# Decoder layer: both rotation products of the paired queries on GpSimd, in pieces of 512 columns, and one of the seven products a place further ahead

## The chip, the core and the metric

The kernel runs on one core of a Trainium2 chip. The metric is the device time of one execution in microseconds (us), the median of several runs. The core's engines work side by side, each through its own queue of instructions in order: TensorE (PE) multiplies matrices, VectorE (DVE), ScalarE (ACT) and GpSimd (POOL) work on elements, and SyncE (SP) mainly starts DMA transfers.

## The reference

One pre-norm decoder layer in fp32 for four sequences of 512 tokens with 512 features. Cut to what matters here:

```python
def rope(v):                       # per head of 64 features
    return v * cos + rotate_half(v) * sin    # rotate_half: (-upper half, lower half)

h  = layernorm(x)
xq = rope((h @ wq).reshape(B, T, 32, 64))    # 32 query heads
xk = rope((h @ wk).reshape(B, T, 8, 64))     # 8 key heads, each for 4 query heads
xv = (h @ wv).reshape(B, T, 8, 64)
p  = softmax(causal(xq @ xk.T / 8))
x  = x + (p @ xv).reshape(B, T, 2048) @ wo

x  = x + quant_dequant(layernorm(x)) @ quant_dequant(ctx_2048).T   # fp8 blocks, per sequence
x  = x + moe(layernorm(x))         # 8 experts of 704, 256 rows each, and a shared expert
```

The quantization takes a scale for each row and block of 128 features, rounds to fp8 and multiplies back.

## The kernel before

**Stages.** The layer norms of the first sequence and the weights come first. Then the attention runs as one loop over 80 rounds, each with two score steps, 160 in all (n = 0 to 159), about 40 for each of the four sequences (b = 0 to 3). The projections, output projections, cross product with the context, and the second and third layer norms of one sequence are pushed in between the score steps of this and the following sequences. The shared expert and the eight experts follow behind the attention, from about 1040 us on in the profile.

**Who decides the order.** The instruction stream is written by Python code that keeps a time model of its own (`Clock`, line 29) and plans against it. A piece of work that may be pushed in is a generator, a job (`add`, line 1239), with the score step from which it may be done, the step by which it must be done and a wish (`want`) that sorts the jobs. What a job yields is its own estimate of the PE time issued, or a condition: `"at"` means not before a planned time, `"done"` not before its own last instruction is planned to have ended, and `"dve", time, cost` that the next instruction is a DVE one of that cost, issued only where the planned DVE queue has room for it. `Fill` (line 1346) picks among the jobs: `upto` fills the gap between two groups of PE work, `need` finishes a job at once where a score step needs its result (line 1498 for the queries). Since everything is planned against the model, a change in one job reorders what is issued behind it.

**The loop.** In each round of the main loop (lines 1750 to 1762), `scores(n + 1)` issues the score products (tile `sc`) one step ahead into four PSUM banks, DVE masks them and takes the maximum (`pm`, `mn`), ACT takes the exponential. `weighted` multiplies finished, transposed probabilities by the values (`av`). `work.upto` fills in jobs. `turned` transposes the probabilities on PE (`pt`) through the same four banks, and DVE or ACT copies them out (`pT`). So `pt` waits until DVE has read the scores out of the bank, and the next `sc` until the copies `pT` are out.

**Other jobs that the text names.** `psk`, `psv`: projections of keys and values. `aT`: the attention's output, scaled by POOL with the reciprocal sums (`rrb`), of which `rr` and `prr` are steps. `py`: products of the output projection (`wo` by `aT`), summed by DVE into `y` and `acc`, and later the product with the context. `qm_x`, `qv_x`, `qq_x`: DVE's steps of the quantization of a row block, which PE then transposes (`ptr_h`) into `h2T`; `qq_c` and `ptr_c` are the same for the context. `T`: differences and sums of the normed rows, which the seven products need.

**Paired queries.** For sequences 1 to 3, `job_q(b, m)` (line 741) computes the queries of four heads at once, m = 0 to 7, 24 such pairs in all. A pair is one tile `t1q` of 128 x 2 x 512: two planes (i = 0, 1), each holding two heads of 64 rows over 512 tokens, of which the score steps read one plane at a time (`qTs[b, 2 * m + i]`). The 2 x 2 block product is done by seven products of 128x256 instead of eight, over prepared sums of weights (`wq`) and rows (`T`), in four PSUM tiles `psq_b_m_0` to `_3`. They lie in the three banks of the kind "mm", which the other projections use too; the first tile is kept open (`kept_open`) until its second half is written. ACT copies the first product into the pair's tile and DVE adds the others to it.

Then comes the rotation. With X the pair, `rt[:, 0]` the cosines and `rt[:, 1]` the signed sines (each 128 x 512, the same for both planes), the kernel forms R2 = X * rt1 (tile `t2q`) and X * rt0 (in place, in `t1q`). `swap` (line 677) exchanges the half-heads of R2 by four DMAs on SP's queue into tile `tsq`, and POOL adds `tsq` to `t1q`, one plane at a time, which makes the plane ready for the scores. There is one tile `t2q` and one `tsq`, so one pair turns at a time; the set `turning` holds it, and `need` finishes a pair that stands in the way first. Queries of sequence 0 (`job_q1`) and the keys (`job_k`) go through `rotated` (line 682), which works on single 128x512 tiles and is the same in both kernels.

All instructions are recorded at the helper's line, L284, so the profile is read by tiles.

Of the kernel before, what the change touches and what calls it, by code (L numbers as in the profile page):

```python
# [11 lines left out]
ALU = mybir.AluOpType  # L12
# [296 lines left out]
def decoder_layer(  # L309
# [18 lines left out]
    clock = Clock()  # L328
    nc = Engines(clock, tc.nc)
# [56 lines left out]
    def places(kind):  # L386

        shut = [
            (place_free(kind, i), clock.used[held[kind, i]][1] if (kind, i) in held else 0, i)
            for i in range(PLACES[kind])  # L390
            if not clock.used.get(held.get((kind, i)), ((kind, i) in held,))[0]
            and (kind, i) not in kept_open
        ]
        return [i for *_, i in sorted(shut)]

    def bank(kind, name, dt=F32, i=None):
        if i is None:
            i = places(kind)[0]
        t = psum.tile([P, 512], dt, tag=f"{kind}{i}", name=name)
        held[kind, i] = t.tensor.name  # L400
        return t
# [218 lines left out]
    gpsimd = nc.gpsimd.tensor_tensor  # L620
# [56 lines left out]
    def swap(ts, t2):  # L677
        for i in range(4):
            o = i ^ 1
            nc.sync.dma_start(out=ts[i * HH : (i + 1) * HH], in_=t2[o * HH : (o + 1) * HH])  # L680
# [39 lines left out]
    turning = set()  # L720

    def pair_tile(b, m):
        return am1.tile([P, 2, T], F32, tag="qT", bufs=4, name=f"t1q_{b}_{m}")

    def turn_tiles(b, m):
        t2 = pj.tile([P, 2, T], F32, tag="t2", name=f"t2q_{b}_{m}")
        ts = pj.tile([P, 2, T], F32, tag="ts", name=f"tsq_{b}_{m}")
        return t2, ts
# [12 lines left out]
    def job_q(b, m):  # L741

        w = wts["q", m]
        a11, a12, s3, a22, s1, s2, s4 = (w[:, i] for i in range(7))
        t1, t2, t3, t4, b11, b21, b22 = Ts[b]

        def product(ps, i, w, x):
            for k in range(2):
                nc.tensor.matmul(
                    ps[:, i * WB : (i + 1) * WB], w[:, k, :], x[:, k, :], start=k == 0, stop=k == 1  # L750
                )

        name = f"q_{b}_{m}"
        add2 = nc.vector.tensor_tensor
        p0 = bank("mm", f"ps{name}_0")
        mine = next(x for x in held if held[x] == p0.tensor.name)
        kept_open.add(mine)
        product(p0, 0, a11, b11)
        Xp = pair_tile(b, m)
        X = Xp.rearrange("p i (h t) -> p (i h) t", h=2)  # L760
        nc.scalar.copy(X[:, 3, :], p0[:, 0:WB])
        yield 860
        p1 = bank("mm", f"ps{name}_1")
        product(p1, 0, a12, b21)
        yield 860
        product(p1, 1, s2, t2)
        halves = lambda ps: ps.rearrange("p (h t) -> p h t", h=2)
        twice = lambda x: x.unsqueeze(1).to_broadcast([P, 2, WB])
        add2(X[:, 0:2, :], halves(p1), twice(X[:, 3, :]), ALU.add)
        yield 860  # L770
        product(p0, 1, s3, t3)
        kept_open.discard(mine)
        add2(X[:, 2, :], p0[:, WB:T], X[:, 1, :], ALU.add)
        yield 860
        p2 = bank("mm", f"ps{name}_2")
        product(p2, 0, s1, t1)
        add2(X[:, 1:4:2, :], twice(p2[:, 0:WB]), X[:, 1:3, :], ALU.add)
        yield 860
        p3 = bank("mm", f"ps{name}_3")
        product(p3, 0, s4, b22)  # L780
        yield 860
        product(p3, 1, a22, t4)
        over["ps" + name] = clock.at
        add2(X[:, 1:3, :], halves(p3), X[:, 1:3, :], ALU.add)
        rot = lambda i: rt[:, i, :].unsqueeze(1).to_broadcast([P, 2, T])
        yield 860
        while turning:
            yield -0.05
        turning.add(m)
        R2, ts = turn_tiles(b, m)  # L790
        yield "dve", clock.begun(R2.tensor.name), 1.2
        nc.vector.tensor_tensor(R2, Xp, rot(1), ALU.mult)
        yield "dve", 0, 1.2
        nc.vector.tensor_tensor(Xp, Xp, rot(0), ALU.mult)
        yield "at", clock.wrote(R2)
        swap(ts, R2)
        yield "done"
        for i in range(2):
            gpsimd(Xp[:, i, :], Xp[:, i, :], ts[:, i, :], ALU.add)
            qTs[b, 2 * m + i] = Xp[:, i, :]  # L800
        turning.discard(m)

    def job_v(b, c, j):
        if not j:
            vs[b, c] = am1.tile([P, TB, HV], F32, tag="v", bufs=3, name=f"v_{b}_{c}")
        ps = bank("mm", f"psv_{b}_{c}_{j}")
        for i in range(2):
            t0 = (2 * j + i) * P
            for k in range(KC):
                nc.tensor.matmul(  # L810
                    ps[:, i * HV : (i + 1) * HV],
                    hTs[b][:, k, t0 : t0 + P],
                    wts["v", c][:, k, :],
                    start=(k == 0),
                    stop=(k == KC - 1),
                )
                if k % 2 and (i, k) != (1, KC - 1):
                    yield 860
        nc.scalar.copy(
            vs[b, c][:, 2 * j : 2 * j + 2, :],  # L820
            ps.rearrange("p (i n) -> p i n", i=2),
        )
        yield 860
# [413 lines left out]
    jobs = []  # L1237

    def add(due, cost, key, gen, *after, want=None):

        jobs.append(Job(due, cost, key, gen, after, want))

    MM4, MM7 = 4 * 860, 7 * 860
    for b in range(B):
        z = b * SPB
# [18 lines left out]
        for c in range(2):  # L1264
            for j in range(2):
                if b or c or j:
                    add(
                        z - 16, MM4, ("v", b, c, j), job_v(b, c, j), ("h", b), ("wv", b, c),
                        want=z - 4 + 0.8 * (2 * c + j),
                    )  # L1270
        if not b:
            for m in range(2 * NG):
# [2 lines left out]
        for a in range(NG):  # L1275
            za = z + 10 * a
            if za:
# [8 lines left out]
                    want=za - 4.5 - 2 * early,  # L1286
                )
            for r, due in enumerate((-17, -12)):
                m = 2 * a + r
                want = 4 * r - 3.2 if a < NG - 1 or b == B - 1 else 1.6 * r - 3.5  # L1290
# [28 lines left out]
            if not n:  # L1319
# [8 lines left out]
                want=za + ((21, 21, 17, 16.5) if b < B - 1 else (22, 19.5, 18, 16.5))[a],  # L1328
# [17 lines left out]
    class Fill:  # L1346
# [91 lines left out]
        def need(self, n, key):  # L1438

            while self.now is not None and key not in over:  # L1440
                self.now = self.step(self.now, n)
            if key in over:
                return
            if isinstance(key, str):
                key = (key[2], *map(int, key.split("_")[1:]))
            job = next(job for job in jobs if job.key == key)
            for k in job.after:
                self.need(n, k)
            jobs.remove(job)
            self.urgent = True  # L1450
            while job:
                for other in [x for x in jobs if turning and x.key[0] == "q" and x.key[2] in turning]:
                    jobs.remove(other)
                    while other:
                        other = self.step(other, n) or (jobs.remove(other) or other if other in jobs else None)
                job = self.step(job, n) or (jobs.remove(job) or job if job in jobs else None)
            self.urgent = False
# [191 lines left out]
    rt = pj.tile([P, 2, T], F32, name="rt")  # L1649
# [521 lines left out]
    _, b, j = units[-1]  # L2171
    for k, lo, hi, py in down_last(gTs[b], se["w"][1], j, f"ys_{b}_{j}"):
        i = b * TB + j + k
# [63 lines left out]
```

## Time and profile before

| | |
|---|---|
| median of 3 runs | 1524.3 us (1522.41 to 1524.41) |
| the profiled execution's own time | 1527.95 us |
| its span in the trace | 1526.2 us |
| its mean granted TensorE clock | 0.995 |
| PE busy | 1500.5 us (98%) |
| DVE, ACT, POOL busy | 928.6, 611.8, 598.8 us |
| PE's share of the chain that ended last | 91% |
| DVE's products `t2q<-t1q,rt`, 128x1024, 24 times | 32.6 us |
| DVE's products `t1q<-t1q,rt`, 128x1024, 24 times | 33.9 us |
| POOL's sums `t1q<-t1q,tsq`, 128x512, 64 times | 84.2 us |

How to read it: the profile is of one execution on the chip. Busy times are sums over an engine's instructions; the span runs from the first to the last recorded instruction, and the profiled execution's own time is a little longer than it. "A <- B" for a wait means that engine A stood idle until B released it; the releaser is inferred and is the last of several. The granted clock is the share of full speed at which TensorE was allowed to run. The 64 sums on POOL are 48 of the paired queries and 16 of sequence 0.

### The profile page before, as it was taken

The numbers are of one execution on the slowest core, as the hardware profiler recorded it, in microseconds if no ns is written. First come the engines' busy times: TensorE is split into PE (matmuls) and PEld (weight loads), VectorE is DVE, ScalarE is ACT, GpSimd is POOL, SyncE is SP. The second block draws the span as 40 slices with busy tenths as digits, with TensorE's granted clock in tenths as the row PEclk, the third lists the DMA queues.
The fourth block names the chain that finished last, engine by engine and source line by source line (L and its number), as shares of the span: only waits on it lengthen the run. The fifth ranks groups of instructions, "written<-read, shape, count | busy, mean of one in ns | idle before, by whom it ended". The sixth has DMA issues, their size and how long they took to land.

```text
span 1526.2 us, 23127 instructions
## 1 busy us (share of the span) xinstructions
PE 1500.5 (98%) x7742; PEld 961.8 (63%) x7745; DVE 928.6 (61%) x2666; ACT 611.8 (40%) x1756; POOL 598.8 (39%) x617
## 2 busy tenths in 40 slices
PE   8999999999999999999999999999999999999999
PEld 5655465756556675655657565655456788868864
DVE  4365635558777666978657687765855554434434
ACT  3554544545455544545455455455111322111100
POOL 2342431103253231334323224423644267776723
PEclk9999999999999999999999999999999999999999
DMA  5575552435352553534334353454051353466526
GB/s 138 161 232 179 172 157 70 139 108 137 88 142 56 156 175 99 146 94 135 111 108 155 112 146 87 131 167 154 27 184 46 108 187 134 160 218 214 201 70 220
DMA packets 120872, 210.73 MB, mean 138 GB/s; under 512 B 16689, under 2 KB 48689, under 8 KB 120241
## 3 DMA queue, kind: packets, MB, share of 16 engines
q1 hardware_dynamic: 116256, 199.03, 43.2%
q0 software_dynamic: 2560, 8.39, 1.6%
q10 hardware_dynamic: 1936, 1.84, 0.4%
q8 instruction: 61, 1.00, 0.3%
q14 instruction: 59, 0.48, 0.1%
HBM read 144.98 MB, written 34.87 MB: 118 GB/s over the span
## 4 chain that ended last, share of the span: by engine, by line
PE 91%; DVE 6%; ACT 1%; issue 1%; DMA 1%; POOL 0%; SPq 0%; DVEq 0%; ACTq 0%; POOLq 0%
PE py L284 14%; PE psq L284 12%; PE p_s L284 9%; PE p_e L284 9%; PE sc L284 9%; PE av L284 9%; PE pt L284 8%; PE ys L284 5%; PE epy L284 5%; PE psv L284 4%; PE psk L284 3%; PE ptr_h L284 1%; ACT pm L284 1%; DVE pm L284 1%; DMA wq<-wsum 1%
## 5 line engine op out<-in xcount | busy, mean ns | idle before, releaser
L284 ACT ACTIVATE pm<-pm,mn 128x256 f32<-128x256 f32 (+3 forms) x512 | 280.8, 549 | 248.7 <-DVE mn L284 248.7
L284 DVE CUSTOM_DVE_ANT_0 pm<-sc,mask 128x256 f32<-128x256 f32 (+3 forms) x512 | 216.7, 486 | 53.4 <-PE sc L284 53.0
L284 PE MATMUL py<-wo,aT 128*128 128x512 f32 x512 | 242.3, 605 | 0.8 <-DVE acc L284 0.8
L284 ACT COPY pT<-pt 128x512 f32<-128x512 f32 (+3 forms) x325 | 130.7, 450 | 136.2 <-PE pt L284 122.5
L284 POOL TENSOR_TENSOR aT<-aT,rrb 128x512 f32<-128x512 f32 x64 | 86.5, 1366 | 245.2 <-DMA rrb<-rrd 208.6
L284 PE MATMUL sc<-kT,t1q 64*128 64x128 f32 (+3 forms) x1024 | 165.1, 451 | 4.8 <-DVE mn L284 2.8
L284 PEld LDWEIGHTS pt<-ident,pm 128*128 128x128 f32 x1280 | 144.4, 141 | 32.1 <-issue 21.1
L284 POOL TENSOR_TENSOR t1q<-t1q,tsq 128x512 f32<-128x512 f32 x64 | 84.2, 1332 | 198.7 <-DMA tsq<-t2q 139.2
L284 PE MATMUL pt<-ident,pm 128*128 128x128 f32 x1280 | 155.3, 274 | 3.7 <-DVE mn L284 3.5
L284 PE MATMUL av<-pT,v 128*64 128x512 f32 (+3 forms) x1024 | 152.4, 439 | 0.2 <-ACT pT L284 0.2
L284 PEld LDWEIGHTS py<-wo,aT 128*128 128x128 f32 x512 | 92.5, 192 | 94.8 <-issue 87.2
L284 DVE COPY pT<-pt 128x256 f32<-128x256 f32 (+3 forms) x187 | 78.6, 444 | 102.4 <-PE pt L284 64.9
L284 PEld LDWEIGHTS av<-pT,v 128*64 128x64 f32 x1024 | 68.4, 136 | 106.8 <-issue 95.2
L284 PE MATMUL psq<-hT,wq 128*128 128x256 f32 (+1 forms) x416 | 132.1, 450 | 0.4 <-ACT h2T L284 0.2
L284 POOL TENSOR_TENSOR acc<-acc,y 128x512 f32<-128x512 f32 x64 | 83.1, 1302 | 124.6 <-DVE y L284 122.7
L284 PEld LDWEIGHTS sc<-kT,t1q 64*128 64x128 f32 x1024 | 85.9, 188 | 70.9 <-issue 44.8
L284 PEld LDWEIGHTS psq<-hT,wq 128*128 128x128 f32 x416 | 76.0, 190 | 36.0 <-issue 27.3
L284 ACT ACTIVATION_READ_ACCUMULATOR pm<-pm,mn 128x1 f32 x512 | 95.5, 187 | 0.0
L284 PE MATMUL psq<-T,wq 128*128 128x256 f32 x384 | 94.7, 383 | 0.8 <-ACT t1q L284 0.8
L284 DVE TENSOR_TENSOR t1q<-psq,t1q 128x512 f32<-128x512 f32 x96 | 59.8, 623 | 49.9 <-PE psq L284 44.0
L284 DVE TENSOR_TENSOR acc<-py,acc 128x512 f32<-128x512 f32 x64 | 43.9, 687 | 68.2 <-PE py L284 67.7
L284 PE MATMUL ys<-slot_s,gT 128*128 128x512 f32 (+3 forms) x204 | 83.0, 588 | 1.7 <-DVE gT L284 1.7
(239 smaller groups left out, 2304.7 us busy)
## 6 DMA issues: line engine op xcount, KB each, us to landing
wq<-wsum SPq DMA_DIRECT2D x24, 896.0 KB, 4.9
slot_e<-in_L_ffn_W_dram SPq DMA_DIRECT2D x16, 1280.0 KB, 8.6
rrb<-rrd SPq DMA_DIRECT2D x64, 256.0 KB, 4.2
wo<-in_L_attn_wo_dram SPq DMA_DIRECT2D x15, 1024.0 KB, 5.4
tsq<-t2q SPq DMA_DIRECT2D x96, 128.0 KB, 2.8
slot_e<-in_L_ffn_W_dram SPq DMA_DIRECT2D x8, 1408.0 KB, 6.2
kT<-t1k SPq DMA_DIRECT2D x60, 128.0 KB, 2.4
wsum<-wq SPq DMA_DIRECT2D x8, 896.0 KB, 4.2
```

Source lines behind the costliest of these rows:

```text
L284: got = call(*args, **kw)
```

## The change

The two rotation products of `job_q` go from DVE, one 128x1024 instruction each, to POOL, two 128x512 instructions each. The two for R2 are issued ahead of the swap, the two in place behind its DMAs. The conditions on room in DVE's queue fall away; the first product instead waits until the tile of R2 is planned to be free. Among the seven products the one of the first sums (s1 by t1, into `psq_2`) is issued one place further ahead, before the second product of the first tile (s3 by t3), so that the two sums which read them come together. The set `turning` names a pair by sequence and number in place of the number alone. The `want` of the value projections is written in another form with the same value.

```diff
         yield 860
+        p2 = bank("mm", f"ps{name}_2")
+        product(p2, 0, s1, t1)
+        yield 860
         product(p0, 1, s3, t3)
         kept_open.discard(mine)
         add2(X[:, 2, :], p0[:, WB:T], X[:, 1, :], ALU.add)
-        yield 860
-        p2 = bank("mm", f"ps{name}_2")
-        product(p2, 0, s1, t1)
         add2(X[:, 1:4:2, :], twice(p2[:, 0:WB]), X[:, 1:3, :], ALU.add)
...
         while turning:
             yield -0.05
-        turning.add(m)
+        turning.add((b, m))
         R2, ts = turn_tiles(b, m)
-        yield "dve", clock.begun(R2.tensor.name), 1.2
-        nc.vector.tensor_tensor(R2, Xp, rot(1), ALU.mult)
-        yield "dve", 0, 1.2
-        nc.vector.tensor_tensor(Xp, Xp, rot(0), ALU.mult)
+        yield "at", clock.begun(R2.tensor.name)
+        for i in range(2):
+            gpsimd(R2[:, i, :], Xp[:, i, :], rt[:, 1, :], ALU.mult)
         yield "at", clock.wrote(R2)
         swap(ts, R2)
+        for i in range(2):
+            gpsimd(Xp[:, i, :], Xp[:, i, :], rt[:, 0, :], ALU.mult)
         yield "done"
         for i in range(2):
             gpsimd(Xp[:, i, :], Xp[:, i, :], ts[:, i, :], ALU.add)
             qTs[b, 2 * m + i] = Xp[:, i, :]
-        turning.discard(m)
+        turning.discard((b, m))
...
-                        want=z - 4 + 0.8 * (2 * c + j),
+                        want=z - 4 + 0.8 * j + 1.6 * c,
...
-                for other in [x for x in jobs if turning and x.key[0] == "q" and x.key[2] in turning]:
+                for other in [x for x in jobs if turning and x.key[0] == "q" and x.key[1:] in turning]:
```

The changed program issues the same number of PE instructions as before. On DVE there are 48 products fewer and nine copies `pT` more, on ACT those nine copies fewer, on POOL 96 products more; SP issues as many DMAs. From the first paired query on (about 230 us) the order of the other work shifts with it.

## The prediction

> **What bounds the kernel now.** I read the busy shares first, then the chain that ended last, then what TensorE (PE) waits for, and only then the rows of the instructions that change.
>
> ```profile
> PE 1500.5 (98%) x7742; PEld 961.8 (63%) x7745; DVE 928.6 (61%) x2666; ACT 611.8 (40%) x1756; POOL 598.8 (39%) x617
> ...
> PE 91%; DVE 6%; ACT 1%; issue 1%; DMA 1%; POOL 0%; SPq 0%; DVEq 0%; ACTq 0%; POOLq 0%
> ```
>
> PE is busy for 1500.5 of 1526.2 us, so all its idle time is 25.7 us. VectorE (DVE) and GpSimd (POOL) have room on average, 61% and 39%. Taking 66 us from DVE therefore gives nothing by itself: only PE's waits can be won or lost. Most of those in the attention part end on DVE (columns: waiting engine and tile, releaser, total us, times, longest):
>
> ```profile
> PE pt L284 <- DVE mn L284: 3.5, 2, 2.2
> PE ptr_h L284 <- DVE qq_x L284: 3.1, 2, 2.0
> ...
> PE sc L284 <- DVE pT L284: 1.8, 1, 1.8
> ...
> ```
>
> The timeline at the longest of them shows whether the changed products stand in DVE's queue ahead of what PE waits for (start, duration, instruction, in brackets the idle time before it).
>
> ```profile
> 433.64 2.17 DVE L284 TENSOR_TENSOR t1q<-t1q,rt 128x1024 f32<-128x1024 f32 x1
> 438.67 3.10 PE L284 MATMUL pt<-ident,pm 128*128 128x128 f32 x16 [2.19 <-DVE mn L284]
> 703.27 1.21 DVE L284 TENSOR_TENSOR t2q<-t1q,rt 128x1024 f32<-128x1024 f32 x1
> 705.29 1.09 PE L284 MATMUL sc<-kT,t1q 64*128 64x512 f32 x3 [1.83 <-DVE pT L284]
> 734.82 0.40 PE L284 MATMUL ptr_h<-ident_b,qq_x 128*128 128x128 bf16 x4 [2.03 <-DVE qq_x L284]
> ```
>
> At 438 and 705 they do. A wait costs more than itself when the clock drops behind it. The table of windows shows one such drop (columns: window, length, then busy time of PE, weight load, DVE, ACT and POOL, granted clock, DMA share, GB/s):
>
> ```profile
> 440.00:444.00 4.00, 3.97 (x11) 2.31 (x12) 3.93 (x14) 3.39 (x12) 1.88 (x2) 0.57 0.48 162
> ```
>
> PE is busy for 3.97 of 4 us there, at a granted clock of 0.57: a loss of 1.7 us (0.43 x 4). The waits at 34, 438.67, 705.29 and 1108.58 have such a drop behind them, those at 106.60, 646.27 and 734.82 don't. The Trainium skill ("TensorE: Matmul & The Clock Gate", "What's actually happening") has the clock fall after an idle window of about 3.4 us; the trace shows it after 2.19 us, so here the measurement decides.
>
> **The change part by part.** The prices come from these rows (lines by form: busy us, mean ns, then idle time before; tile rows: min/median/max ns, first and last start).
>
> ```profile
> L284 DVE TENSOR_TENSOR t1q<-t1q,rt 128x1024 f32<-128x1024 f32 x24 | 33.9, 1413 | 0.4
> L284 POOL TENSOR_TENSOR t1q<-t1q,tsq 128x512 f32<-128x512 f32 x64 | 84.2, 1332 | 198.7 <-DMA tsq<-t2q 139.2 <-DVE t1q L284 26.0 <-DVE mn L284 20.7
> ...
> L284 DVE TENSOR_TENSOR t2q<-t1q,rt x24: 1159/1223/2309, 239.2 to 978.2; 128x1024 f32<-128x1024 f32 x24
> L284 POOL TENSOR_TENSOR t1q<-t1q,tsq x64: 1262/1276/2258, 27.2 to 985.8; 128x512 f32<-128x512 f32 x64
> ```
>
> *Moved work.* DVE loses 24 x 1.36 (the t2q products by form, 32.6 us busy) + 24 x 1.41 = 66.5 us. POOL gains 24 x 4 = 96 products of 128x512. No row shows a POOL multiplication of this shape; the nearest is its addition of the same shape and sources, 1.27, so 96 x 1.27 = 122 us. POOL is busy for 251 of the 810 us from 230 to 1040 where these pairs are rotated, so it has room. The second products (61 us) follow the issue of the swap; POOL stood idle for 139.2 us behind exactly that swap (tsq<-t2q), which hides them. The first products lie on the pair's path: 2 x 1.27 in place of 1.22, so 1.3 us later per pair.
>
> *DVE's waits.* In the program's order of the changed kernel the transposes of step 62 still follow the scores of step 63 with nothing between, but the 2.17 us product is no longer in DVE's queue ahead of them: -0.9 of the wait (2.19 less the 1.30 that the same bare order costs at 106.60), -1.7 of clock, and +1.0 because the scores of step 65, which had 5.5 us of output projection (py) before them, now follow bare: -1.6. At step 103 likewise: -1.2 (the product's 1.21), -1.7, +1.3 for a new bare place: -1.6.
>
> *The quantize waits.* Here the nearest rows speak against the change, since they show what POOL's work does to DVE's:
>
> ```profile
> 382.97 0.43 DVE L284 TENSOR_SCALAR qm_x<-qm_x 128x512 f32<-128x512 f32 x1
> 383.43 0.69 DVE L284 TENSOR_TENSOR qv_x<-qv_x,qm_x 128x512 f32<-128x512 f32 x1
> ...
> 730.04 1.38 DVE L284 TENSOR_SCALAR qm_x<-qm_x 128x512 f32<-128x512 f32 x1
> 731.45 1.63 DVE L284 TENSOR_TENSOR qv_x<-qv_x,qm_x 128x512 f32<-128x512 f32 x1
> ```
>
> The first pair ran alone, the second beside POOL: 0.95 us more each. By the order, though, the PE work between a quantized row and its transposes grows for most of them (12.3 to 19.9 us and 10.2 to 20.5 us for two of batch 3; 10.0 unchanged for the first of batch 0), so the waits 2.0 + 0.7 (at 734.82) + 0.7 + 0.3 + 0.7 = 4.4 us should go: -4.4. For one or two quantize instructions slowed where the distance did not grow I add +1.0 (bounds 0 and 4, four such instructions). The Trainium skill ("SBUF — State Buffer", "SBUF: two separate sides") calls the port pair that the two engines share an exclusive lock, held for a whole instruction, taken by a DVE instruction with two SBUF sources. By it each of the four instructions could wait a whole POOL product, about the bound of 4, and the sum would be 3 us worse.
>
> *The last pair.* For most pairs the PE work between the last product (psq) and the first score that reads the pair stays over 15 us. Pair 7 of batch 3 falls from 33.8 us to about 6.2: behind its last product only sixteen transposes, four program lines of py (eight records) and two scores of pair 6 remain, by the same records of before 1.75 (986.03 to 987.78) + 3.60 + about 0.9.
>
> ```profile
> 977.51 0.69 DVE L284 TENSOR_TENSOR t1q<-psq,t1q 128x512 f32<-128x512 f32 x1 [1.03 <-PE psq L284]
> 978.23 1.94 DVE L284 TENSOR_TENSOR t2q<-t1q,rt 128x1024 f32<-128x1024 f32 x1
> 980.25 2.41 SPq L284 DMA_DIRECT2D tsq<-t2q  x4
> 984.59 2.50 POOL L284 TENSOR_TENSOR t1q<-t1q,tsq 128x512 f32<-128x512 f32 x2 [5.49 <-PE py L284]
> 986.03 1.91 PE L284 MATMUL pt<-ident,pm 128*128 128x128 f32 x16
> 987.78 3.60 PE L284 MATMUL py<-wo,aT 128*128 128x512 f32 x8
> ```
>
> The pair then needs DVE's add 0.69, two POOL products 2.52, product end to sum 4.42 (980.17 to 984.59, over the four swap DMAs) and one sum 1.26: 8.9 us against 6.2, a wait of 2.7. POOL is also due to scale aT at that time, so I add one such instruction (1.3): +4.0, and +1.7 for the clock, since the wait exceeds 2 us. Bounds: 2 without POOL's other work and with a quick swap, 10 when the swap takes its slowest (8.2 instead of the median 2.4). The few waits just behind (0.4 + 0.2 + 0.2) would be absorbed, as the other engines run ahead while PE stands: -0.8. Net +4.9.
>
> *The rest.* With the product of the first sums issued before p0's second one, three of the three "mm" banks are held for one place longer. PE's waits before psq total 1.2 us, so 0, bounds -1.2 and +1.2. The two sums that follow go back to back on DVE: 0. SP issues the same 682 DMAs; its queue now stands behind a POOL product instead of a DVE one, 1.3 us longer 24 times, in front of weight loads that come 20 us ahead of use: 0. Keying the rotations by (batch, pair) lets a pair of the next batch wait for its own alone: 0. The changed `want` is the same number. If other pairs than the last came late (the pair with the least room keeps 15 us against 13), it would cost up to 4.
>
> Sum: -1.6 - 1.6 - 4.4 + 1.0 + 4.9 = -1.7 us on 1527.95, the profiled execution's own time (span 1526.2). The median of 1524.3 is 3.65 below that, so 1524.3 - 1.7 = 1522.6.
>
> **The rivals.** *POOL's rotations come late* (slower). One place: the scores that read a pair just rotated. If POOL still works on aT or T when a pair's sums end, both first products queue behind it, then the swap, then the sums. For pair 7 of batch 3 the wait becomes 9 to 10 + 1.7 instead of 4.0 + 1.7, and the two pairs of batch 2 with 15 to 17 us cost 2 more: 1522.6 + 5.5 + 2 = 1530. It decides from a pair latency of about 13 us. For it: POOL's idle time ahead of its sums ends on the swap, so the swap is already the pair's slow part. Against it: measured latencies of 12.5 to 18 us mostly lie below the room.
>
> *The last pair is hidden and DVE's relief is all won* (faster). If the swap lands in 2 us and POOL is free, the last wait is about 1 without a clock drop, and the last pair's +4.9 becomes +0.2 (1.0 less the 0.8 absorbed), the sum -1.7 - 4.7 = -6.4: 1517.9. For it: the fastest swap lands in 1.9 us, and POOL is idle for most of the attention part. Against it: 8.9 against 6.2 leaves 2.7 even at the swap's usual time.
>
> *The change does little*: the moved products lay beside PE, the new bare places cost what the old ones did, quantize waits return elsewhere: 1524.3. The busy share of PE, 98%, speaks for it, the reordering of everything behind 230 us against it.
>
> **How the numbers follow.** Forecast 0.40, late rotations 0.33, hidden last pair 0.19, no change 0.08. About 0.2% (3 us) is what a measurement of this kernel can tell from no change: faster means below 1521.25, slower above 1527.35. The forecast's own range, from its unknown terms, is 1518 to 1528: about 0.38 of it is faster, 0.50 the same, 0.12 slower. The late case is slower in 0.9 of it, the same in 0.1; the hidden one faster. Faster 0.15 + 0.19 = 0.34; same 0.20 + 0.03 + 0.08 = 0.31; slower 0.05 + 0.30 = 0.35. The range 1515 to 1533 leaves out about a tenth on either side: a swap at its slowest beside late POOL above, further waits lost to DVE's relief below.
>
> **What would show it.** In the profile after: 48 t2q and 48 t1q products on POOL near 1.27 each, none on DVE; no clock drop near 440 and 706; ptr_h no longer waiting on qq_x; and one PE wait of sc on POOL t1q of 3 to 5 us in the last attention steps. It is wrong if that wait is missing or far longer, if sc waits on POOL at other pairs, if the quantize waits remain, or if POOL's products take clearly more than 1.3.

## The result: slower by 22 us, and the profile after

The changed kernel takes 1545.7 us (median of 4 runs, 1540.0 to 1549.4) against 1523.6 beside it: a ratio of 1.0139, 95% interval 1.0117 to 1.0161. The forecast was 1522.6, with a range up to 1533. The profile after is of the execution of 1549.41 us. Its page, the lines of the busy shares and of the chain that ended last:

```profile
PE 1508.4 (97%) x7740; PEld 963.6 (62%) x7745; DVE 896.8 (58%) x2627; ACT 605.9 (39%) x1745; POOL 703.2 (45%) x713
...
PE 87%; DVE 9%; ACT 2%; issue 1%; DMA 0%; POOL 0%; SPq 0%; DVEq 0%; ACTq 0%; POOLq 0%
```

Of the span's growth from 1526.2 to 1547.7 us, 13.6 us are idle time of PE (25.7 to 39.3) and 7.9 us are PE busy for longer over the same work. Some 4.8 of these 7.9 are a lower granted clock: summed over windows of 10 us, the share below full speed comes to 7.9 us before and 12.7 after. DVE, relieved of products that took 66.5 us, is only 31.8 us less busy (928.6 to 896.8), so its other work took about 35 us more (some 4 of them are the nine copies `pT` that it took over). PE's waits after (waiting engine and tile, releaser, total us, times, longest):

```profile
PE sc L284 <- DVE mn L284: 3.2, 1, 3.2
PE sc L284 <- POOL t1q L284: 3.0, 1, 3.0
PE psq L284 <- ACT cT L284: 2.7, 1, 2.7
PE psq L284 <- ACT h2T L284: 2.7, 1, 2.7
PE ptr_c L284 <- DVE qq_c L284: 1.8, 1, 1.8
PE pc L284 <- DVE r_before L284: 1.5, 1, 1.5
PE py L284 <- DVE cmx L284: 1.5, 1, 1.5
...
PE pt L284 <- DVE mn L284: 1.3, 1, 1.3
...
PE pc L284 <- DVE r_oh L284: 1.0, 1, 1.0
...
PE ptr_h L284 <- DVE qq_x L284: 0.9, 1, 0.9
```

The waits that the change was forecast to remove are indeed smaller: `ptr_h <- qq_x` went from 3.1 to 0.9, `pt <- mn` from 3.5 to 1.3 (the rest is the one at 106, ahead of the change), `sc <- DVE pT` of 1.8 is gone. In their place stand many others, spread over tiles that had hardly waited; the first row stood there before too, with 2.8. Two of those shown name ACT. What lay ahead of the one at 423 is in the timeline after (start, duration, instruction, idle time before it):

```profile
411.40 2.99 POOL L284 TENSOR_TENSOR t2q<-t1q,rt 128x512 f32<-128x512 f32 x2 [6.19 <-DVE t1q L284]
411.49 0.36 DVE L284 TENSOR_SCALAR qm_x<-qv_x 128x512 int32<-128x512 int32 x1
411.89 1.37 DVE L284 TENSOR_SCALAR qm_x<-qm_x 128x512 f32<-128x512 f32 x1
413.29 1.64 DVE L284 TENSOR_TENSOR qv_x<-qv_x,qm_x 128x512 f32<-128x512 f32 x1
414.35 3.39 POOL L284 TENSOR_TENSOR t1q<-t1q,rt 128x512 f32<-128x512 f32 x2
414.97 1.64 DVE L284 TENSOR_TENSOR qq_x<-qv_x,qm_x 128x512 bf16<-128x512 f32 x1
416.53 1.25 DVE L284 TENSOR_TENSOR sxw<-sf_c,sf_x 128x16 f32<-128x16 f32 x1
...
418.90 0.28 DVE L284 CUSTOM_DVE_ANT_0 pm<-sc,mask 128x128 f32<-128x128 f32 x1
...
419.22 0.40 ACT L284 ACTIVATE pm<-pm,mn 128x128 f32<-128x128 f32 x1 [6.73 <-DVE mn L284]
...
423.17 0.57 ACT L284 COPY h2T<-ptr_h 128x512 bf16<-128x512 bf16 x1
...
423.79 1.13 PE L284 MATMUL psq<-T,wq 128*128 128x256 f32 x4 [2.68 <-ACT h2T L284]
```

GpSimd runs its four pieces one behind the other from 411.40 to 417.74. In that time DVE gets through five short instructions, 1.37, 1.64, 1.64 and 1.25 us for the last four, which alone take 0.43, 0.69, 0.69 and 0.17. So the mask and maximum come late, ACT stands still for 6.73 us (3.00 in the same order without pieces, shown below), and its queue then has six exponentials and a copy ahead of the copy of `h2T` that frees PE's bank. The releaser that the wait names, ACT, is three steps behind the cause.

### The profile page after: what moved, and what is told of

Same layout as the page of the kernel before. It is cut to its first block, busy times and chain, and to the rows that moved or that the text cites. A ratio compares the mean times of both kernels' runs of the same rounds, so it can differ in the third digit from the quotient of the medians.

```text
span 1547.7 us, 23123 instructions
## 1 busy us (share of the span) xinstructions
PE 1508.4 (97%) x7740; PEld 963.6 (62%) x7745; DVE 896.8 (58%) x2627; ACT 605.9 (39%) x1745; POOL 703.2 (45%) x713
## 4 chain that ended last, share of the span: by engine, by line
PE 87%; DVE 9%; ACT 2%; issue 1%; DMA 0%; POOL 0%; SPq 0%; DVEq 0%; ACTq 0%; POOLq 0%
PE py L284 14%; PE psq L284 12%; PE p_e L284 9%; PE sc L284 9%; PE p_s L284 9%; PE pt L284 8%; PE av L284 8%; PE epy L284 5%; PE ys L284 5%; PE psv L284 4%; PE psk L284 3%; DVE pm L284 1%; ACT pm L284 1%; PE ptr_h L284 1%; DVE pT L284 1%
## 5 line engine op out<-in xcount | busy, mean ns | idle before, releaser
L284 ACT COPY pT<-pt 128x256 f32<-128x256 f32 (+3 forms) x316 | 127.5, 451 | 137.2 <-PE pt L284 121.8
L284 POOL TENSOR_TENSOR aT<-aT,rrb 128x512 f32<-128x512 f32 x64 | 81.0, 1279 | 194.3 <-DMA rrb<-rrd 152.3
L284 DVE COPY pT<-pt 128x256 f32<-128x256 f32 (+3 forms) x196 | 81.9, 444 | 132.4 <-PE pt L284 77.1
L284 POOL TENSOR_TENSOR t1q<-t1q,tsq 128x512 f32<-128x512 f32 x64 | 80.8, 1280 | 119.4 <-DMA tsq<-t2q 100.9
L284 POOL TENSOR_TENSOR t2q<-t1q,rt 128x512 f32<-128x512 f32 x48 | 61.5, 1303 | 66.1 <-DVE t1q L284 65.2
```

The lines of the kernel that those rows point to most:

```text
L284: got = call(*args, **kw)
```

## The experiments

The kernel plans its own order, so an edit also moves everything behind it. In the runs named "plan" the order is held fixed: the instruction is issued on the one engine while the planner's model is told of the other. PE's queue then has the same instructions in the same order as in the kernel named, and so have the other engines for all work not edited. Differences below are to the runs of before beside them. Theory P is that GpSimd's pieces hold up VectorE; B, that the product issued ahead waits for a bank; R, that the new order of the other work costs by itself; L, that the pair's path is longer; A and U, that pieces cost the same each or far more in a row.

**The engine alone, in the order of before.**

```diff
-        nc.vector.tensor_tensor(R2, Xp, rot(1), ALU.mult)
+        for i in range(2):
+            tc.nc.gpsimd.tensor_tensor(R2[:, i, :], Xp[:, i, :], rt[:, 1, :], ALU.mult)
+        clock.spend("vector", "tensor_tensor", (R2, Xp, rot(1), ALU.mult), {})
# and the second product in the same way
```

> The order of every instruction is that of before; only the 48 rotation products are taken out of VectorE's queue and issued as 96 pieces to GpSimd, in the places where the planner had them. Theory P (port: GpSimd's pieces hold up VectorE's short instructions, and PE waits behind chains of these): slower than before by 6 to 12 us, with the router's and quantization's short instructions at 0.5 to 1.3 us beside the pieces. Theory B (bank: the product issued ahead asks for a third bank that still holds a transpose) and theory R (the new order of the other work is what costs): within 3 us of before, or faster, since VectorE loses 66 us of work.

1545.1 us, ratio 1.0125 (1.0110 to 1.0141): +19.1, more than the 6 to 12 that P had expected, and far outside the 3 of B and R. With every other instruction in its old place, the move to GpSimd alone loses nearly as much as the whole change. At the quantization of 382 the kernel before has, beside the two rows of 0.43 and 0.69 us that the prediction showed:

```profile
382.52 0.41 DVE L284 TENSOR_SCALAR qm_x<-qv_x 128x512 int32<-128x512 int32 x1
...
384.16 0.69 DVE L284 TENSOR_TENSOR qq_x<-qv_x,qm_x 128x512 bf16<-128x512 f32 x1
...
384.90 0.40 PE L284 MATMUL ptr_h<-ident_b,qq_x 128*128 128x128 bf16 x4 [1.07 <-DVE qq_x L284]
```

This kernel has:

```profile
381.39 2.67 POOL L793 TENSOR_TENSOR t2q<-t1q,rt 128x512 f32<-128x512 f32 x2
...
381.82 1.12 DVE L284 TENSOR_SCALAR qm_x<-qv_x 128x512 int32<-128x512 int32 x1
382.98 1.37 DVE L284 TENSOR_SCALAR qm_x<-qm_x 128x512 f32<-128x512 f32 x1
384.03 3.11 POOL L797 TENSOR_TENSOR t1q<-t1q,rt 128x512 f32<-128x512 f32 x2
384.38 1.63 DVE L284 TENSOR_TENSOR qv_x<-qv_x,qm_x 128x512 f32<-128x512 f32 x1
386.05 1.64 DVE L284 TENSOR_TENSOR qq_x<-qv_x,qm_x 128x512 bf16<-128x512 f32 x1
...
387.75 0.50 PE L284 MATMUL ptr_h<-ident_b,qq_x 128*128 128x128 bf16 x3 [4.51 <-DVE qq_x L284]
```

The same four steps take 5.76 us in place of 2.22, and PE's wait behind them is 4.51 in place of 1.07.

**The order of after, products back on VectorE, the place among the seven back, and both.**

```diff
# products: nc.vector as before, the model told of four GpSimd pieces
# place:
-        product(p2, 0, s1, t1)
+        product(p0, 1, s3, t3, (p2, 0, s1, t1))   # last: what the model is told
-        product(p0, 1, s3, t3)
+        product(p2, 0, s1, t1, (p0, 1, s3, t3))
```

> The order of after, but the products go back to VectorE as 48 instructions of 128x1024 in the places where the planner had GpSimd's. Theory P: 8 to 12 us faster than after (about 1535), and the wait of the scores on the last pair is shorter. Theory B: waits of psq of 2.7 us on ACT stay, 1542 to 1548. Theory R: 1542 to 1548 as well.

1550.1 us, ratio 1.0169 (1.0145 to 1.0193).

> The order of after, products on GpSimd, but in each pair the product of the first sums and the second product of the first tile trade places again, with nothing else moved. Theory B: the two waits of psq of 2.7 us (on ACT h2T at 423 and ACT cT at 838) and their clock drops go: 6 to 9 us faster than after, about 1538. Theories P and R: within 2 us of after.

1549.0 us, ratio 1.0140 (1.0122 to 1.0158).

> The order of after for all other work, with both parts of the change undone (products on VectorE, product of the first sums back behind). Theory R: still slower than before by 10 us or more, 1534 to 1545, since only the order of the other work is left of the change. Theories P and B together: within 4 us of before, 1522 to 1528.

1545.8 us, ratio 1.0133 (1.0114 to 1.0152).

Trading the places back won nothing. In its trace the two waits of psq are still there under another name, `psq <- ACT t1q`, 5.6 us in two: the second product of the first tile now waits for the same ACT queue at the same two places. B falls: with the products on GpSimd the place in the seven is worth nothing. With the products on VectorE, the kernel with the place back is 4.4 us faster (1545.8 against 1550.1), at the edge of the two intervals. The two runs with the products on VectorE missed theory P's numbers and lie near those of R, but they told little: their order was planned with no room for products on VectorE. Their largest wait is of the scores on late pairs (`sc <- POOL t1q`, 10.0 us in the one, 6.3 in the other, 3.0 after), so they mix the price of the order with products in bad places. Runs without any product leave that out.

**No products, in either order.**

```diff
-        nc.vector.tensor_tensor(R2, Xp, rot(1), ALU.mult)
+        clock.spend("vector", "tensor_tensor", (R2, Xp, rot(1), ALU.mult), {})
# the second product, and GpSimd's pieces in the order of after, in the same way; the swap reads Xp
```

> The order of before with the 48 rotation products of the paired queries left out on every engine (the swap moves the unrotated pair instead, so the queries are not rotated). It prices the products' whole presence on VectorE in the order of before. Theory P (the order of before is sound, and the time went to GpSimd's pieces holding up VectorE): 3 to 8 us faster than before, the waits of 2.2 and 1.8 us with the products ahead of them gone. Theory R: about the same.

1520.2 us, ratio 0.9964 (0.9949 to 0.9979): -4.9.

> The order of after with the 96 pieces left out in the same way. Theory P: the pieces are most of the loss, so 15 to 22 us faster than after, about 1525 to 1530. Theory R (the new order of the other work costs by itself): only 3 to 10 us faster than after, 1535 to 1543. The difference between this kernel and the one without products in the order of before is the price of the order alone: under 5 us by P, 10 us or more by R.

1525.2 us, ratio 0.9998 (0.9986 to 1.0010): +0.1.

This splits the result. From before, taking the products away gives -4.9; the order of after costs +5.0; the 96 pieces then cost about 20.5 (1525.2 to 1545.7; 21.5 by the ratios, since after was measured elsewhere). The pieces' presence is most of the loss, as P has it, and the new order about a quarter, as R has it. DVE's busy time tells the same: 865.4 us without products and 897.4 with the pieces in the order of before, 861.1 and 896.8 in the order of after, 32 and 36 us of hold-up over the same DVE instructions. PE's own idle time grows by 14.7 and 13.8 us in the two pairs of profiles; the rest is PE busy for 8.0 and 10.0 us longer, 4.5 and 7.8 of them at a lower granted clock, summed as above.

At the place of the wait at 423, the order of after without pieces has no wait of psq. VectorE's four steps take 0.43, 0.69, 0.69 and 0.17 us there, and ACT waits for 3.00 us in place of 6.73. The chain that ended last has 5% on DVE in place of 9%:

```profile
413.59 0.40 ACT L284 ACTIVATE pm<-pm,mn 128x128 f32<-128x128 f32 x1 [3.00 <-DVE mn L284]
...
PE 92%; DVE 5%; ACT 1%; DMA 1%; issue 1%; SPq 0%; POOL 0%; DVEq 0%; ACTq 0%; POOLq 0%
```

POOL's share of that chain is 0% with and without the pieces. So a rival that no theory named, that GpSimd's own results come late because the pieces stand in its queue, is not where the time went.

**Only the second, only the first products, in the order of before** (the other stays on VectorE; edits as above).

> The order of before, the first products stay on VectorE, and only the second ones (48 pieces, behind the first and beside the swap) go to GpSimd. If the loss of 19 us with both on GpSimd is the hold-up of VectorE (theory P), about half of it stays, +7 to +12 us over before, with quantization chains beside the pieces still two to three times as long. If it is the pair's longer path from its sums to the swap (theory L), nearly none stays, within 3 us of before, since these pieces lie beside the swap.

1527.2 us, ratio 1.0012 (1.0002 to 1.0022): +2.1.

> The order of before, only the first products (48 pieces, ahead of the swap) on GpSimd, the second ones on VectorE. Both together cost 19 us, the second alone 2 us. Theory A (the two parts add up, the first being the costly one by its place): +15 to +19 us. Theory U (what counts is how long GpSimd runs without a gap, since each VectorE instruction of a chain then meets a piece of its own: four pieces in a row, not two): +2 to +8 us, so that the two parts alone together cost far less than both at once.

1531.9 us, ratio 1.0056 (1.0041 to 1.0071): +6.7.

The second alone missed P's +7 to +12 and by itself speaks for L. But the two parts alone make 8.8 us and together 19.1, and 6.7 is in U's range. The timeline of the kernel with the first products alone shows why:

```profile
378.86 2.68 POOL L793 TENSOR_TENSOR t2q<-t1q,rt 128x512 f32<-128x512 f32 x2
379.29 1.12 DVE L284 TENSOR_SCALAR qm_x<-qv_x 128x512 int32<-128x512 int32 x1
380.44 1.37 DVE L284 TENSOR_SCALAR qm_x<-qm_x 128x512 f32<-128x512 f32 x1
381.85 0.69 DVE L284 TENSOR_TENSOR qv_x<-qv_x,qm_x 128x512 f32<-128x512 f32 x1
382.58 0.69 DVE L284 TENSOR_TENSOR qq_x<-qv_x,qm_x 128x512 bf16<-128x512 f32 x1
...
383.32 0.40 PE L284 MATMUL ptr_h<-ident_b,qq_x 128*128 128x128 bf16 x4 [1.02 <-DVE qq_x L284]
```

Two pieces hold two of the four steps (3.87 us in all), four hold all four (5.76). PE's slack here takes up the first, so its wait is 1.02, and not the second: 4.51.

**Smaller pieces: 192 of 256 columns.**

```diff
+            for h in (slice(0, WB), slice(WB, T)):
+                tc.nc.gpsimd.tensor_tensor(R2[:, i, h], Xp[:, i, h], rt[:, 1, h], ALU.mult)
```

> The order of before, both products on GpSimd as in the run with +19 us, but in 192 pieces of 256 columns, some 0.75 us each. Theory P with the hold-up lasting a whole piece: short VectorE instructions wait up to 0.75 instead of 1.27 us each, the chain of four quantization steps of 5.8 us falls to 4 to 4.5 us, and the loss to 10 to 15 us. Theory L: the pair's path grows by 24 x 4 x 0.1 us of extra fixed cost, and the loss stays at 19 us or grows.

1530.5 us, ratio 1.0032 (1.0019 to 1.0045): +5.3, of 19.1 with whole pieces and better than the 10 to 15 expected, though the pair's path is no shorter and POOL is busier (723.3 us against 705.7). Theory L falls by this as the main cause in this order. DVE's busy time falls from 897.4 to 883.2, and the four steps are at

```profile
380.61 0.58 DVE L284 TENSOR_SCALAR qm_x<-qv_x 128x512 int32<-128x512 int32 x1
381.22 0.83 DVE L284 TENSOR_SCALAR qm_x<-qm_x 128x512 f32<-128x512 f32 x1
382.09 1.09 DVE L284 TENSOR_TENSOR qv_x<-qv_x,qm_x 128x512 f32<-128x512 f32 x1
383.22 1.10 DVE L284 TENSOR_TENSOR qq_x<-qv_x,qm_x 128x512 bf16<-128x512 f32 x1
```

3.60 us in all; the last three lose 0.4 each instead of 0.95. What an instruction loses goes with the length of the piece that it meets.

> The order of after with the 96 pieces cut into 192 of 256 columns. If the hold-up of VectorE by whole pieces is what the change lost, the pieces' price in this order falls as it did in the order of before (from 25 to 10 us over the order without products), so from 20 to about 8: 1531 to 1536, 10 to 14 us faster than after. If the loss came from the longer path of a pair or from the order, 1543 to 1548 as after.

1543.1 us, ratio 1.0113 (1.0095 to 1.0131): +17.9, only 4 us better than after, with intervals that overlap. The expectation failed. VectorE is held almost as long as with whole pieces: it is busy for 895.6 us, against 896.8 with them and 861.1 without any, where in the order of before the cut had saved 14 us. The router's chain of the trace shows one reason. Without pieces (order of after) its steps from 564.09 to the end of `r_before` take 1.65 us; in after they end 4.64 us behind the first, and with the halved pieces 4.9 us:

```profile
564.51 0.58 DVE L284 TENSOR_TENSOR r_oh<-r_lg,r_mx 128x32 f32<-128x32 f32 x1
565.00 2.77 POOL L800 TENSOR_TENSOR t1q<-t1q,rt 128x256 f32<-128x256 f32 x4
565.12 0.65 DVE L284 TENSOR_TENSOR r_oh<-r_oh,ie 128x32 f32<-128x32 f32 x1
565.81 0.19 DVE L284 TENSOR_REDUCE r_ex<-r_oh 128x4 f32<-128x32 f32 x1
...
567.74 1.25 POOL L284 TENSOR_TENSOR t1k<-t1k,tsk 128x512 f32<-128x512 f32 x1
567.84 1.58 DVE L284 TENSOR_TENSOR r_before<-r_before,r_oh 128x8 f32<-128x8 f32 x3
...
569.48 0.41 PE L284 MATMUL pc<-r_before,ones 128*128 128x32 f32 x2 [2.55 <-DVE r_before L284]
```

With whole pieces GpSimd was done, `t1k` included, after four held steps. Here five steps meet smaller pieces, and the last ones run into GpSimd's next instruction, `t1k`, of 512 columns.

**What is left in the order of after.** Without the second pieces, and with all of GpSimd's instructions on 512 columns cut in two:

```diff
+    def gpsimd(out, x, y, op):
+        if math.prod(out.shape[1:]) == T:
+            h = out.shape[1] // 2
+            for s in (slice(0, h), slice(h, 2 * h)):
+                tc.nc.gpsimd.tensor_tensor(out[:, s], x[:, s], y[:, s], op)
```

> The order of after with the 48 second pieces (X times the cosines) left out and the first ones kept on GpSimd. Without any piece this order took 1525, with all 96 about 1546. Theory U (long runs of GpSimd without a gap do the harm): the first pieces alone cost 3 to 9 us, 1528 to 1534. Theory A (each piece costs the same): half of the 20 us, 1534 to 1537. If the pair's longer path counts, the first pieces carry nearly all of it, 1540 or more.

1532.9 us, ratio 1.0058 (1.0044 to 1.0071): 7.7 us over none, in the range of U. The second pieces, which lie beside the swap and which the prediction took as free, add 13 of the 20.5 us here, on top of the first.

> The order of after with all GpSimd instructions on 512 columns, the 96 pieces among them, cut in two. Cutting the pieces alone gave about 4 of 20 us. If the neighbours' length is what is left (sums, scaling of aT, differences T, which a held chain runs into), another 4 to 8 us, 1534 to 1539. If chains of many short VectorE instructions simply meet one piece after another for as long as GpSimd has work, cutting brings nothing more: 1541 to 1546.

1540.3 us, ratio 1.0105 (1.0089 to 1.0120): 2.8 us better than with only the pieces cut, less than expected if the neighbours' length were what is left. PE's wait `pc <- r_before` is still 3.0 us. So in this order cutting gives 5 to 8 us in all (5.4 between the medians, 7.7 between the differences to before). What is left goes with what VectorE still loses. Over the order without pieces it is busy for 13.9 us longer without the second pieces, 29.8 with everything cut, 34.5 with the pieces cut and 35.7 in after; the time is longer by 7.7, 15.1, 17.9 and 20.5 us, between 0.5 and 0.6 us for each us of hold-up. This fits P in the order of after too. How the loss divides between single chains, the last pair and the clock stays open.

**The place in the seven alone, planned anew** (products on VectorE).

> Before with only the product of the first sums moved one place ahead, everything planned anew, products on VectorE. Trading the places back within the order of after changed nothing but the names of the waits, so the place itself should cost nothing; a new order of the other work may: 1524 to 1531. A gain of over 3 us would mean that the place matters after all.

1532.6 us, ratio 1.0065 (1.0045 to 1.0084): +7.4, just above what was expected. The place itself is worth nothing in a fixed order with the products on GpSimd, but it makes the planner choose another order, and that one is worse. Its largest wait is `ptr_c <- qq_c`, 5.3 us in two. An order planned anew can cost as much as what was edited.

**A version that beats both.** Before, with the same cut of all GpSimd instructions on 512 columns and nothing else, in its own order.

> The order of before with the products on VectorE, and every GpSimd instruction on 512 columns (sums of the rotations, scaling of aT, sums of y, quantization's first product, differences T and the shared expert's products) cut into two of half the size. By the hold-up of whole pieces VectorE's stretched instructions of before (quantization at 730, wait of 2.0 us at 734.82) should get shorter: 2 to 5 us faster than before, 1520 to 1523. If the extra fixed cost of some 280 more GpSimd instructions reaches PE, up to 4 us slower.

1520.2 us, ratio 0.9969 (0.9958 to 0.9979): 5.0 us faster than before. DVE is busy for 916.1 in place of 928.6 us though its work is the same, and PE's idle time falls from 25.7 to 20.3. At the quantization beside the differences T, which the prediction showed with 1.38 and 1.63 us and a wait of 2.03, this kernel has:

```profile
723.52 1.78 POOL L625 TENSOR_TENSOR T<-hT,T 128x256 f32<-128x256 f32 x2
723.88 0.83 DVE L285 TENSOR_SCALAR qm_x<-qm_x 128x512 f32<-128x512 f32 x1
724.75 1.10 DVE L285 TENSOR_TENSOR qv_x<-qv_x,qm_x 128x512 f32<-128x512 f32 x1
...
727.03 0.40 PE L285 MATMUL ptr_h<-ident_b,qq_x 128*128 128x128 bf16 x4 [0.41 <-DVE qq_x L285]
```

> The order of before with all GpSimd instructions cut in two (1520 us without more) and the second products also moved to GpSimd in pieces of 256 columns. The second products alone in pieces of 512 cost 2 us, VectorE is relieved of 34 us: between 2 us faster and 3 us slower than the cut alone, 1518 to 1523.

1524.4 us, ratio 1.0000 (0.9987 to 1.0013), above the 1518 to 1523 expected. Moving even half of the products to GpSimd, cut small, gives the gain back.

## Why the prediction was wrong, by its own steps

**The step that failed is the price of contention.** It was +1.0 (bounds 0 and 4) for "four such instructions" of the quantization, and 0 for everything else beside 122 us of added GpSimd work. The row it was taken from was right: 0.95 us more per instruction is what held instructions lose after as well. The count was wrong. Short VectorE work between SBUF tiles is held in many places, reductions apart: the router's `r_lg` goes from a mean of 184 to 741 ns, the layer norm's `rsb <- veb` from 425 to 938. In sum VectorE loses 32 to 36 us to the pieces, PE stands idle for about 14 us more, and the pieces cost about 20.5 us in place of the 1.0.

The Trainium skill ("SBUF — State Buffer", "SBUF: two separate sides") calls the shared ports an exclusive lock for the whole instruction. The trace agrees, with losses of 0.95 to 1.1 us beside pieces of 1.28 and about 0.4 beside those of half the size (2.77 us for four). The prediction weighed the rule, and then applied it to four instructions (four whole pieces of 1.27 us would be 5.1, not 4) where the sum over GpSimd's whole added time was called for.

**"The second products are hidden by the swap": wrong.** They are hidden on POOL, where the idle time behind the swap went down (`t1q <- tsq` from 139.2 to 100.9 us). These 139.2 us hold the swaps of sequence 0 too; from 230 us on, where the pairs are, it is 71.7 us before and 26.1 after. But their cost is on another engine: 13 us in the order of after, on top of the first products.

**"For most of them the PE work between a quantized row and its transposes grows, so the waits go": right, and too narrow.** Those waits went. The hold-up reached PE by queues that the prediction did not follow: VectorE's maximum, then ACT's exponentials, then the copies that free PE's banks (psq, 2.7 us twice).

**The order as such** was looked at place by place and summed to nothing outside the places named. It costs 5.0 us. The wait at step 103 went with its clock drop, as forecast. The one at step 63 went, but the scores of step 65, priced at +1.0 without a drop, wait for 1.46 us at 443.86 with a granted clock of 0.58 over the 4 us from 445 on, again a loss of 1.7. So the sign "no clock drop near 440" failed, and this step gave about 0.7 in place of 1.6. Others of 0.9 to 1.8 us came, behind chains that the prediction had no view of, as `ptr_c` at 1084. They stand in the order of after without pieces as well.

**What was right.** The pieces take 1.28 us each (61.5 + 61.9 us for 96). For their price the prediction said that no row shows a GpSimd multiplication of this shape; one did, `aT<-aT,rrb` of 128x512, with a mean of 1366 ns before. VectorE's products gave PE little: 4.9 us with all of them gone. The place in the seven is worth 0 with the products on GpSimd. The last pair's wait was forecast as 4.0 with a clock loss of 1.7; it is 3.0 (0.25 in the same order without pieces), and the table of windows of after (window, length, busy PE, PEld, DVE, ACT, POOL, granted clock, DMA share, GB/s) shows 0.67 over 5 us, a loss of 1.65:

```profile
423.00:430.00 7.00, 6.21 (x29) 5.43 (x30) 3.06 (x5) 2.88 (x8) 4.50 (x5) 0.76 0.87 203
570.00:590.00 20.00, 17.48 (x65) 9.06 (x64) 12.78 (x36) 6.44 (x20) 7.81 (x7) 0.83 0.34 80
1031.00:1036.00 5.00, 3.88 (x15) 1.81 (x16) 2.37 (x12) 3.43 (x11) 2.29 (x2) 0.67 0.34 82
```

The other two rows are drops behind the new waits at 423 and at 573 to 575, 1.7 and 3.4 us, which no step had. The reason given for the drop behind the last pair, a wait over 2 us, is not what the rows of before show: there a drop follows the wait of 1.83 at 705.29 and none follows that of 2.03 at 734.82.

**The slower rival** had the sign and not the mechanism. It put the loss at scores that wait for late pairs; those waits are 3.0 us in all, at one pair.

## What to carry to other kernels

An engine with idle time is not free to use if its work holds up another. Price moved work first by what its neighbours lose, over the whole time that the new instructions run (here 123 us of pieces cost VectorE 32 to 36 us), and follow a late step through every queue behind it. Where chains of short VectorE steps feed PE, try shorter GpSimd instructions. Here they won back 14 of 19 us in one order and 5 to 8 of 20.5 in the other. Fewer in a row helped too: either half of the pieces alone cost 2.1 and 6.7 us, both 19.1. And where a planner orders the work, separate the edit from the new order by holding the order fixed.

## What the runs showed of the hardware

A VectorE instruction of 128x16 or 128x32 elements, 0.17 to 0.19 us alone, takes up to 1.3 us beside GpSimd's pieces. Not all are held: reductions (`r_ex`, 0.19 in both) and work on PSUM (the mask, 0.69 for 512 columns) keep their time. Cutting 279 of the 617 GpSimd instructions of before in two made the whole kernel 5 us faster, though GpSimd itself was busy for 47 us more (598.8 to 645.5).
